# A four-layer graph network on one core: two PSUM slots skipped, sums ordered behind the first pairs, small inputs joined, five checks moved to a later layer

## The chip, the cores and the metric

The kernel runs on one core of a Trainium2 chip. The metric is the device time of one execution in microseconds; the time before is the median of three executions. The profile comes from one further execution, whose own time is given beside its span below.

## What is computed

Four graph layers are applied in turn to 4096 nodes of 64 features with one dense 0/1 matrix `adj` (4096 x 4096, float32). After each layer stands the same residual and normalisation. Cut to what matters:

```python
# layer 0
deg = clip(sum(adj, 1) + 1, 1);  h = (adj @ x + x) / deg
z = relu(concat([x, h]) @ W + b);  out = z / max(norm(z), 1e-12)
# layers 1 and 3 (hyperbolic; c from r, and 1)
left, right = logmap0(x) @ w_att[:D], logmap0(x) @ w_att[D:]
att = sigmoid(left[:, None] + right[None, :] + b_att) * adj
out = proj(expmap(x, einsum('ij,ijd->id', att, logmap(x_i, x_j))))
# layer 2: the last edges of a row weigh 1, 1/2, 1/4, ...
w = mask * 0.5 ** (k - pos);  out = w @ (x @ weight) + bias
# after each: x = layernorm(x + out)
```

## The kernel before

**Tiling.** The host lays `adj` out so that one load (`load(s, g)`, line 718) brings 128 x 2 x 1024 floats, 1 MB: two blocks of 128 neighbours (blocks 2g and 2g+1) for one group `s` of 1024 nodes. There are four groups, `GROUPS` = 3, 2, 1, 0, and sixteen `g` in each, 15 down to 0, so each layer reads 64 MB in 64 loads. All loads are issued by SP's queue into six buffers (`loads`). A buffer is free when TensorE, and the check where there is one, have read it. The matrix products read the upper halves of the floats as bf16.

**Checks.** The fast path holds only if every entry of `adj` is 0 or 1. `check` (line 884, instruction at L886) reads one load on VectorE and counts the entries that are neither. Each of the 64 loads of a sweep is checked once: in layer 0, or, where `checked_later(s, g)` says so, when the same load passes again in layer 2 (`load_2`).

**Layer 0** (from line 1581). For each group, TensorE multiplies each load with the bf16 parts of x (`first`, `third`, L1598) into four accumulators of one PSUM bank each, two `sums` and two `counts`, out of a pool `m0_ps` of six slots. At the group's end `nc.scalar.copy` empties them, in the last group VectorE two of the four (L1628, L1636). What follows for each node (row work) is written as Python generators: `end_0` makes the sums per node by matmuls with `sum_w` and `count_w` (L1544, L1545) and goes on to the normalisation (`norm_rows`) and to what layer 1 needs (`prepare`). `later` puts such a generator into a list, and `tick(n)` moves the lists on by n places, so the row work of one group lies between the pairs of the next. Inside `tc.manual_schedule(engines=FIXED)` TensorE and ScalarE keep the order in which the program names their instructions; VectorE's order is the scheduler's, with row work held behind the checks and pairs before it (`mark`). Outside such blocks the scheduler orders all engines.

**Layers 1 and 3** (`attend`, line 1134). For each block j of 128 neighbours, six matmuls (L1170, L1173, L1176) fill a z tile of two banks, one of three in pool `p_ps`; ScalarE makes the sigmoid (L1190) and a square (L1193), VectorE combines them (L1196 for each block, L1199 for two), and TensorE adds the result up (L1148). Two blocks, one `g`, are called a pair of blocks here. The pool `p_ps` opens when the pools of layer 0 are closed, so its z tiles lie in banks that layer 0 used. In the first sweep of layer 1 the last group's `end_0` runs beside the pairs, partly on GpSimd; the pairs of g = 3 to 0 need its outcome (`need((layer, 2 * g // WB))`). Line 1623 applies a sigmoid to one element, which loads ScalarE's table.

**Layer 2** (`wide_pass`, `narrow_pass`). Groups 3 and 2 are taken at once, then 1, then 0, in fixed order on TensorE and ScalarE. Counting matmuls (L1790), an exponential (L1797) and sums (L1756, L1802) for each block; the checks left from layer 0 run here on VectorE, and so does the row work of `end_2`, `norm_rows` and `prepare` for layer 3, whose results TensorE turns (L1040) and spreads (L1124).

**Small inputs.** Weights and biases come by fourteen transfers from ScalarE's queue near the start: five into `given` (L93), `w0` twice (L96, L1525), two attention rows (L859), `w2` three times (L1613 to L1615), and the rest in a fallback block that is entered only if the checks fail.

Of the kernel before, what the change touches and what calls it, by code (L numbers as in the profile page):

```python
# [10 lines left out]
F32 = mybir.dt.float32  # L11
# [3 lines left out]
AF = mybir.ActivationFunctionType  # L15
# [4 lines left out]
P = 128  # L20
N = 4096
D = 64
NB = N // P
W = 512
# [37 lines left out]
def gnn_stack_kernel(  # L62
# [4 lines left out]
    w0: bass.AP,  # L67
    b0: bass.AP,
    r1: bass.AP,
    w_att1: bass.AP,  # L70
    b_att1: bass.AP,
    w2: bass.AP,
    b2: bass.AP,
    w_att3: bass.AP,
    b_att3: bass.AP,
# [10 lines left out]
    w0_sb = const.tile([2 * D, D], F32, name="w0_sb")  # L86
    w2_sb = const.tile([D, D], F32, name="w2_sb")
# [3 lines left out]
    for src, at in ((b0, 0), (b2, D), (b_att1, 2 * D), (b_att3, 2 * D + 1), (r1, 2 * D + 2)):  # L91
        n = src.shape[0]
        nc.scalar.dma_start(given[:, at : at + n], src.rearrange("(o n) -> o n", o=1))  # L93
    one_row = const.tile([1, P], F32, name="one_row")
    V.memset(one_row, 1.0)
    nc.scalar.dma_start(w0_sb, w0)  # L96
# [475 lines left out]
    def stream(fits):  # L572

        with ExitStack() as st:
# [149 lines left out]
            def checked_later(s, g):  # L724

                return g in (0, 1, 2, 3, 5, 7, 9, 11) or (s in GROUPS[:2] and g in (4, 6))
# [126 lines left out]
            def att_rows(w_att, n):  # L853

                t = att_space[:, n * 4 * D : (n + 1) * 4 * D].rearrange(
                    "o (u k d) -> o u k d", u=2, k=2
                )
                src = w_att.rearrange("(u d) o -> o u d", u=2)
                nc.scalar.dma_start(t, src[:, :, None, :].to_broadcast([1, 2, 2, D]))  # L859
                return t  # L860
# [272 lines left out]

            def attend(layer, s, rate, then):

                left_b = left_bs[s]
# [19 lines left out]
                for g in reversed(range(NB // 2)):  # L1156
# [4 lines left out]
                    for k in (1, 0):  # L1161
# [17 lines left out]
                        if k == 1:  # L1179
# [9 lines left out]
                        sig = sb.tile([P, WW], F32, name="sig", bufs=3)  # L1189
                        nc.scalar.activation(  # L1190
                            sig, left_b, AF.Sigmoid, bias=right[:, j : j + 1]
                        )
# [275 lines left out]
            w2_twice = keep.tile([P, D], F32, name="w2_twice")  # L1468
# [5 lines left out]
            with ExitStack() as lp:  # L1474
# [23 lines left out]
                def constants():  # L1498
# [10 lines left out]
                    V.memset(sum_w[:, D:], 0.0)  # L1509
                    V.tensor_copy(sum_w[D:, :D], w0_sb[D:, :])  # L1510
# [14 lines left out]
                nc.scalar.dma_start(sum_w[:D, :D], w0[D:, :])  # L1525
                att_rows1, att_rows3 = att_rows(w_att1, 0), att_rows(w_att3, 1)
# [5 lines left out]
                def end_0(s, tops):  # L1532
# [3 lines left out]
                    for some in ((0, 1),) if spare else ((0,), (1,)):  # L1536
                        ts = []
                        for h in some:
                            top, low = tops[h]
                            t = take(F32, P, SB, P)  # L1540
                            for k in range(SB):
                                cols = slice(k * P, (k + 1) * P)
                                to = t[:, k, : D + 1]
                                nc.tensor.matmul(to, top[:, cols], sum_w, start=True, stop=False)  # L1544
# [379 lines left out]
```

## Time and profile before

| | us |
|---|---|
| median of three executions | 1049.47 |
| their range | 1048.6 to 1050.73 |
| the profiled execution | 1051.42 |
| its span, first to last instruction | 1049.7 |
| TensorE busy | 977.7 (93%) |
| VectorE busy | 907.8 (86%) |
| ScalarE busy | 751.7 (72%) |
| GpSimd busy | 322.1 (31%) |
| moved by DMA | 271.62 MB |

PE is TensorE, PEld its weight loads, DVE VectorE, ACT ScalarE, POOL GpSimd and SP the engine that issues loads. A "q" behind a name means the engine's sequencer. A row of a group of instructions gives line, engine, operation, output<-inputs, shapes and count, and in brackets how long the engine had been idle and what ended it. A row of windows gives the stretch, its length, each engine's busy time (with instructions), the granted share of TensorE's clock, the share of the DMA engines, and GB/s. The busy share of a whole kernel is an average over four layers with different limits, so most of what follows is read from stretches.

### The profile page before, as it was taken

The page shows a single profiled execution, that of the slowest core. Times are in us where ns is not written, and L with a number is a line of the kernel's source. Part 1 is how long each engine was busy: PE and PEld are TensorE (multiplying, and loading weights), DVE is VectorE, ACT ScalarE, POOL GpSimd, SP SyncE. Part 2 cuts the span into 40 slices and gives each one's busy share as a digit, 9 for nine tenths or more (in the row PEclk, how much of TensorE's full clock was granted, in tenths as well). Part 3 has the DMA queues.
Part 4 walks back from the last instruction along what each step waited for, and adds up shares of the span by engine and source line. Part 5 has one row for each costly group of instructions (what it writes and reads, how often), then busy time and mean ns, then how long its engine had stood idle before and what let it go on. Part 6 is the DMA issues. An engine that isn't in the chain of part 4 may idle for free.

```text
span 1049.7 us, 13606 instructions
## 1 busy us (share of the span) xinstructions
PE 977.7 (93%) x4845; PEld 397.9 (38%) x4845; DVE 907.8 (86%) x1401; ACT 751.7 (72%) x873; POOL 322.1 (31%) x695
## 2 busy tenths in 40 slices
PE   5999997979999999999999999998999999999991
PEld 2455554423333333333333344443333333333330
DVE  7486978789999999999488579858999999999996
ACT  0003123769989888898677688888998898888970
POOL 0011111163055365365210020104501662572660
PEclk9999999999999999999999999999999999999996
DMA  8999999655665566566599998996465666665600
GB/s 339 421 416 407 394 422 381 228 189 177 235 233 203 206 240 208 193 241 229 213 327 353 369 358 308 327 332 231 168 233 199 241 210 205 241 229 186 233 1 24
DMA packets 38580, 271.62 MB, mean 259 GB/s; under 512 B 4710, under 2 KB 4710, under 8 KB 5734
## 3 DMA queue, kind: packets, MB, share of 16 engines
q1 hardware_dynamic: 37728, 270.03, 70.0%
q8 instruction: 40, 0.66, 0.2%
q10 hardware_dynamic: 774, 0.63, 0.2%
q14 instruction: 38, 0.31, 0.1%
HBM read 269.58 MB, written 1.05 MB: 258 GB/s over the span
## 4 chain that ended last, share of the span: by engine, by line
PE 60%; DVE 22%; DMA 6%; POOL 5%; ACT 4%; issue 2%; ACTq 0%; SPq 0%; POOLq 0%; DVEq 0%
PE acc L1148 16%; PE z L1790 11%; PE z L1170 8%; DVE t L1199 7%; PE z L1176 7%; PE z L1173 7%; DVE t L1196 6%; DMA edges<-in_adj_dram 5%; PE z L1802 3%; DVE junk L886 3%; PE acc L1598 3%; PE z L1756 2%; ACT sq L1193 2%; ACT sq L1797 1%; DMA w_twice<-in_L_gnn_weight_dram 1%
## 5 line engine op out<-in xcount | busy, mean ns | idle before, releaser
L1196 DVE SCALAR_TENSOR_TENSOR t<-z,sig 128x1024 f32<-128x1024 f32 x256 | 308.6, 1218 | 24.9 <-ACT sq L1193 22.7
L1193 ACT ACTIVATE sq<-z 128x1024 f32<-128x1024 f32 x256 | 255.5, 1023 | 66.0 <-PE z L1176 31.9
L1199 DVE SCALAR_TENSOR_TENSOR t<-sq,t 128x2048 f32<-128x2048 f32 x127 | 294.5, 2319 | 0.3
L1190 ACT ACTIVATE sig<-left_b,right 128x1024 f32<-128x1024 f32 x256 | 287.0, 1149 | 1.9 <-DVE t L1196 1.0
L1148 PE MATMUL acc<-t,xe 128*64 128x512 f32 x1024 | 255.7, 605 | 16.0 <-DVE t L1199 14.7
L1170 PE MATMUL z<-edges,two_i 128*128 128x512 bf16 x512 | 201.1, 393 | 1.1 <-DVE t L1196 1.1
L1176 PE MATMUL z<-dst,src 74*128 74x512 f16 x512 | 195.1, 381 | 0.0
L1173 PE MATMUL z<-lo_hi,hi_lo 128*128 128x512 f16 x512 | 194.0, 379 | 0.0
L1797 ACT ACTIVATE sq<-z 128x512 bf16<-128x512 f32 (+1 forms) x192 | 138.0, 740 | 39.9 <-PE z L1790 38.7
L1148 PEld LDWEIGHTS acc<-t,xe 128*64 128x64 f32 x1024 | 63.6, 136 | 145.0 <-issue 104.3
L886 DVE SCALAR_TENSOR_TENSOR t<-edges 128x2048 bf16<-128x2048 f32 x36 | 82.4, 2304 | 19.7 <-DMA edges<-in_adj_dram 19.5
L1598 PE MATMUL acc<-edges,first 128*128 128x512 bf16 x256 | 80.2, 394 | 20.5 <-DMA edges<-in_adj_dram 20.0
L1170 PEld LDWEIGHTS <-two_i 128*128 128x128 bf16 x512 | 50.4, 98 | 119.9 <-issue 74.7
L1790 PE MATMUL z<-edges,pass_by 128*128 128x512 bf16 x248 | 86.6, 389 | 6.3 <-ACT sq L1797 5.7
L1790 PE MATMUL z<-edges,enter 128*128 128x512 bf16 x256 | 88.3, 387 | 0.0
L1598 PE MATMUL acc<-edges,third 128*65 128x512 bf16 x256 | 79.5, 391 | 0.0
L1176 PEld LDWEIGHTS <-src 74*128 74x128 f16 x512 | 49.2, 96 | 72.6 <-issue 10.6
L886 DVE SCALAR_TENSOR_TENSOR junk<-edges 128x2048 bf16<-128x2048 f32 x28 | 64.0, 2284 | 11.7 <-DMA edges<-in_adj_dram 11.6
L1173 PEld LDWEIGHTS <-hi_lo 128*128 128x128 f16 x512 | 50.3, 98 | 56.6 <-issue 11.3
L1299 POOL TENSOR_TENSOR w_att<-x,u 128x512 f32<-128x512 f32 x6 | 16.2, 2707 | 149.5 <-ACT u L1293 149.5
L1756 PE MATMUL z<-sq,halves 128*128 128x512 bf16 x128 | 48.0, 377 | 0.2 <-ACT sq L1797 0.2
L1404 ACT COPY x_t<-aux 64x512 f32<-64x512 f32 x8 | 4.6, 576 | 57.5 <-PE aux L1399 57.5
(476 smaller groups left out, 989.4 us busy)
## 6 DMA issues: line engine op xcount, KB each, us to landing
edges<-in_adj_dram SPq DMA_DIRECT2D x256, 1024.0 KB, 4.9
x<-in_x_dram SPq DMA_DIRECT2D x4, 256.0 KB
out_dram<-x ACTq DMA_DIRECT2D x2, 256.0 KB
out_dram<-x SPq DMA_DIRECT2D x2, 256.0 KB
w_sb<-in_L_gnn_W_dram ACTq DMA_DIRECT2D x1, 32.0 KB, 4.8
w_twice<-in_L_gnn_weight_dram ACTq DMA_DIRECT2D x2, 16.0 KB, 7.9
given<-in_L_gnn_b_dram ACTq DMA_DIRECT2D x1, 0.2 KB
given<-in_L_gnn_bias_dram ACTq DMA_DIRECT2D x1, 0.2 KB
```

The lines of the kernel that those rows point to most:

```text
L886: V.scalar_tensor_tensor(junk, a, 0.0, a, ALU.not_equal, ALU.not_equal, accum_out=odd[:, n : n + 1])
L1148: it = nc.tensor.matmul(acc[h * D : (h + 1) * D, :], xe[:, j, :], t[:, k, h * W : (h + 1) * W], start=j == BLOCKS[0], stop=j == BLOCKS[-1],)
L1170: nc.tensor.matmul(half, two_i, edge[:, at : at + W], start=True, stop=False)
L1173: nc.tensor.matmul(half, hi_lo[:, of], lo_hi[:, to], start=False, stop=False)
L1176: last = nc.tensor.matmul(half, src[:, of], dst[:, to], start=False, stop=True)
L1190: nc.scalar.activation(sig, left_b, AF.Sigmoid, bias=right[:, j : j + 1])
L1193: nc.scalar.activation(sq[:, k], zp, AF.Square, bias=ROOT + OFF, scale=-1.0 / UNIT)
L1196: V.scalar_tensor_tensor(ts[k][:, k], zp, 0.0, sig, ALU.max, ALU.mult)
L1199: V.scalar_tensor_tensor(t, sq, HIGH**2, t, ALU.add, ALU.mult)
L1598: nc.tensor.matmul(accs[h][:m], lhs[:, j, :], edge[:, at : at + W], start=j == BLOCKS[0], stop=j == BLOCKS[-1],)
L1790: nc.tensor.matmul(z[:, h : h + W], lhs, rhs[:, h : h + W], start=j == BLOCKS[0], stop=True, skip_group_check=True,)
L1797: weighed[0] = nc.scalar.activation(w, z[:, :n], AF.Exp, bias=-(OFF_EDGE + CUT) * LN2, scale=-LN2)
```

## The change

Four things are done. The first group of layer 0 first takes and gives back two PSUM slots, so that the four accumulators of every group lie two slots further on. In the last `end_0` the first matmul of the sums of each half is ordered behind the last matmul of the pairs traced so far; and the sigmoid of layer 1's first block is made in the last iteration of layer 0, in place of the one-element sigmoid, while `tick` goes five places in the last group. The host joins the weights into one array of 128 x 3 x 64 and the small vectors and attention rows into one row. And `checked_later` sends five more checks to layer 2: g = 8, 6 and 4 of group 0, g = 4 of group 1, and g = 8 of group 2.

```diff
-    for src, at in ((b0, 0), (b2, D), (b_att1, 2 * D), (b_att3, 2 * D + 1), (r1, 2 * D + 2)):
-        n = src.shape[0]
-        nc.scalar.dma_start(given[:, at : at + n], src.rearrange("(o n) -> o n", o=1))
+    nc.scalar.dma_start(given, small[:, : 2 * D + 3])
+    nc.scalar.dma_start(weights_sb, weights)
...
-    nc.scalar.dma_start(w0_sb, w0)
...
-                return g in (0, 1, 2, 3, 5, 7, 9, 11) or (s in GROUPS[:2] and g in (4, 6))
+                more = {0: (4, 6, 8), 1: (4,), 2: (4, 6, 8), 3: (4, 6)}
+                return g in (0, 1, 2, 3, 5, 7, 9, 11) or g in more[s]
...
-                src = w_att.rearrange("(u d) o -> o u d", u=2)
-                nc.scalar.dma_start(t, src[:, :, None, :].to_broadcast([1, 2, 2, D]))
...
+            def sigmoid(layer, s, j):
+
+                early = layer == 1 and j == BLOCKS[0] and s == GROUPS[0]
+                if early:
+                    sig = lefts.tile([P, WW], F32, name="left_b")
+                else:
+                    sig = sb.tile([P, WW], F32, name="sig", bufs=3)
+                nc.scalar.activation(sig, left_bs[s], AF.Sigmoid, bias=right[:, j : j + 1])
+                return sig
...
+                        sig = ahead_of.pop() if ahead_of else sigmoid(layer, s, j)
...
+                    V.tensor_copy(sum_w[:D, :D], weights_sb[:D, 1])
...
-                nc.scalar.dma_start(sum_w[:D, :D], w0[D:, :])
-                att_rows1, att_rows3 = att_rows(w_att1, 0), att_rows(w_att3, 1)
+                nc.scalar.dma_start(att_space, atts_in)
+                att_rows1, att_rows3 = att_rows(0), att_rows(1)
...
+                                one = nc.tensor.matmul(
+                                    to, top[:, cols], sum_w, start=True, stop=False
+                                )
+                                if place[0] == 1 and not k:
+                                    in_order(one.ins, pairs_last[mybir.EngineType.PE])
...
+                        if s == GROUPS[0]:
+                            for _ in range(2):
+                                V.memset(ps.tile([P, W], F32, name="acc")[:1, :1], 0.0)
...
-                                nc.scalar.dma_start(w2_sb, w2)
-                                nc.scalar.dma_start(w2_twice[:D], w2)
-                                nc.scalar.dma_start(w2_twice[D:], w2)
...
-                            tick(4)
+                            if last and g == 0:
+                                ahead_of.append(sigmoid(1, GROUPS[0], BLOCKS[0]))
+                            tick(5 if last else 4)
...
-                            nc.scalar.activation(turned_on, one_row[:, :1], AF.Sigmoid)
```

## The prediction

> **What bounds the kernel now.** I read the slices of the page first, then DMA rate in windows of 5 us, what the load queue (SP) waited for, the timeline where layer 0 turns into layer 1, and last the windows of layer 2.
>
> ```profile
> PE   5999997979999999999999999998999999999991
> DVE  7486978789999999999488579858999999999996
> DMA  8999999655665566566599998996465666665600
> ```
>
> Three regimes: up to slice 7 (layer 0, to 176 us) and again in slices 20 to 27 (layer 2) the DMA share is high; in layers 1 and 3 PE and DVE are both near full and DMA is at six tenths. So a load that comes earlier is worth time in layer 0, a DVE instruction is worth time in layers 1 and 3, and layer 2 (DVE 5 to 9 tenths) has DVE room.
>
> ```profile
> 5.00:10.00 5.00, 3.10 (x8) 1.30 (x9) 4.17 (x8) 0.52 (x1) 0.00 (x0) 1.00 0.86 289
> ...
> 35.00:40.00 5.00, 4.37 (x21) 2.08 (x21) 2.26 (x5) 0.05 (x1) 0.00 (x0) 1.00 1.02 424
> ...
> 80.00:85.00 5.00, 3.76 (x16) 1.54 (x15) 4.89 (x23) 1.66 (x3) 2.40 (x6) 1.00 0.91 338
> ...
> 125.00:130.00 5.00, 3.67 (x16) 1.54 (x15) 4.97 (x11) 0.63 (x2) 1.30 (x4) 1.00 0.97 351
> ...
> 160.00:165.00 5.00, 5.00 (x24) 2.24 (x22) 4.76 (x17) 0.00 (x0) 0.00 (x0) 1.00 0.97 359
> ...
> 180.00:185.00 5.00, 4.37 (x18) 3.56 (x19) 1.19 (x9) 0.59 (x1) 0.00 (x0) 0.55 1.01 426
> ```
>
> The last number is GB/s, the one before the DMA share, before it the granted clock. A good window moves about 420 GB/s. The first 10 us and the windows near 80, 125 and 160 us fall short, and each of the three later ones has DVE at 4.8 to 5.0 of 5. The last row shows PE at clock 0.55: the turn of the layers.
>
> ```profile
> SPq L720 <- DVE junk L886: 93.1, 26, 6.4
> ...
> SPq L720 <- DMA given<-in_L_gnn_b_att_dram: 2.7, 1, 2.7
> SPq L1492 <- DMA xw<-in_L_gnn_att_w_dram: 2.6, 1, 2.6
> SPq L1492 <- DMA given<-in_L_gnn_bias_dram: 2.0, 1, 2.0
> ```
>
> The load queue waits for checks (L886) to free a buffer, and at the start for the landing of small transfers that it has no use for.
>
> ```profile
> 176.56 0.56 ACT L1628 COPY sums<-acc 128x512 f32<-128x512 f32 x1
> ...
> 179.62 0.68 DVE L1628 COPY sums<-acc 128x512 f32<-128x512 f32 x1
> ...
> 180.63 0.66 PE L1544 MATMUL aux<-sum_w,sums 128*128 128x65 f32 x2 [4.11 <-DVE own L1070]
> ...
> 183.65 0.63 PE L1170 MATMUL z<-edges,two_i 128*128 128x512 bf16 x1
> ...
> 187.56 1.23 DVE L1196 SCALAR_TENSOR_TENSOR t<-z,sig 128x1024 f32<-128x1024 f32 x1 [6.33 <-ACT sq L1193]
> ```
>
> PE's layer 0 ends at 176.5. It stands 4.1 us until DVE, held by row work of the group before, has emptied its two accumulators, then does the sums per node, and only at 183.65 the first pair. DVE, which paces layer 1, starts pairs at 187.56.
>
> **The change, part by part.** *Fewer small DMAs.* Five into `given`, two of `w0`, three of `w2`, two attention rows become three (`given`, `weights`, `small`'s rest), all on ACT's queue, where ACT's first instruction is a table load at 9.48. The bytes stay (96 KB of weights), SP's own list of loads too; the fallback block, whose attention loads become four, is not entered. Here a rule speaks against any gain: the Trainium skill, "DMA: Bandwidth & Descriptors", section "Issuing engines are not separate DMA queues", says that transfers from several engines share the same 16 DMA engines and that issuing elsewhere saves only sequencer time. By it the removed issues (0.24 to 0.72 us each in the timeline, on an idle ACT) are worth 0. The rows above differ: SP itself waited 2.0 + 2.7 + 2.6 us for them, its second load went out at 6.75 in place of some 2. I follow the rows. Bytes missing up to 20 us against 420 GB/s, from 2 us on: (420 x 3 − 875) + (420 − 289) x 5 + (420 − 372) x 5 = 385 + 655 + 240 = 1280 KB, or 3.0 us. The cover is the six load buffers: the eleventh load was released by a check at 30.0 us with 6.6 us of transfers still queued, so DVE does not take the place of the DMA. DVE also loses a wait of 1.95 us for `w_twice`, and gains one copy of 0.2 us. I take 2.7 (0 to 3.3).
>
> *Checks moved.* 28 in layer 0 become 23 (group 2 loses g=8, group 1 g=4, group 0 g=8, 6, 4), at 2.29 us each. At 77.6 and 161.0 to 171.1 they are the DVE instruction that releases the next load (issues at 79.94, 163.40, 168.87, 171.21 follow their ends by 0.2 us). Missing bytes: 75 to 85 us 480 KB = 1.1 us; 120 to 130 us 635 KB = 1.5 us, but these hang on the checks of g=8 and 6, which stay, so half; 160 to 174 us some 600 KB = 1.4 us, with a little of the dip before it. Taken: 1.0 + 0.7 + 1.6 = 3.3 us (1 to 5.2). DVE also has the row work of group 1 done 6.9 us sooner, which kept its copies until 179.0. `tick(5)` spreads that row work over 13 places fewer out of 64, about 8 us earlier in PE's and ACT's fixed order; behind it stand the layer's last matmuls. With DVE 6.9 us sooner I cost it at 0, bound 0 to 3 us; its cover is PE's own waits for edges (0.5 us each at 168.3 and 170.8).
>
> *Rotation, order, early sigmoid.* Two one-element memsets (0.06 us each) turn the six accumulators by two, so that the first z tile lies in banks that the last group does not use; the sums per node are ordered behind the last matmul of the first pair. Before: 187.56 − 176.5 = 11.1 us from PE's end to the first L1196. After: PE 6 matmuls at the full-clock step of 0.217 = 1.3 us, with no idle time that lowers the clock; ACT two copies (0.5 each by their steps), one 1.0 us turn copy, one square 1.0 = 3.0 us; DVE two copies 1.4 us. The longest is ACT, 3.0 us: gain 8.0. Edges do not hold it: the first six loads of layer 1 were issued between 169.3 and 175.9, 2.5 us apart in landing against 4.6 us of DVE per pair of blocks (2 x 1.2 + 2.3, the means of L1196 and L1199). The early sigmoid takes its 1.15 us and table load (1.28, already there for `turned_on`) out of this stretch; without it the gain is 6.9 or less. Queued behind the new order: the 16 matmuls of the sums, 3.5 us, and with them the POOL chain that ends with `right` of group 0 at 253 us. They start some 3 us behind the first DVE pair, just as now (190.49 against 187.56), so chain and pairs move together. Taken 8.0 (4 to 9).
>
> *Layer 2 takes five checks*, 5 x 2.29 = 11.5 us of DVE.
>
> ```profile
> 640.00:650.00 10.00, 9.68 (x53) 4.57 (x52) 9.66 (x41) 8.49 (x16) 0.00 (x0) 1.00 0.90 313
> 650.00:660.00 10.00, 8.56 (x49) 4.87 (x47) 8.33 (x23) 8.90 (x17) 0.00 (x0) 1.00 0.82 306
> ...
> 690.00:700.00 10.00, 9.93 (x68) 5.07 (x67) 4.77 (x10) 8.81 (x15) 0.00 (x0) 1.00 0.88 293
> ```
>
> Group 2's goes into 540 to 550, and is caught up by 570, where DVE idles 2.6 us. Group 1's lies ahead of `left` (L1080 at 645.6), which PE needs at 647.43 in its fixed order: 2.3 − 1.6 slack = 0.7 us. Group 0's three, 6.9 us, meet idle times of 2.0 and 5.2 us at 686.9 and 699.4; two lie ahead of L1002 (686.88), which PE needs at 692.48, so 4.6 us against 4.9 of slack. A second rule speaks against the move: "GPSIMD Engine Reference", Key points: POOL contends with a DVE instruction that has two SBUF inputs, as a check has. The chain of waits shows it: `146.70 2.96 POOL sq L1559`, 1.04 when undisturbed, under a check. By the rule each check may hold POOL 2.3 us, 11.5 in all; but POOL's last copies for that turn end at 676.1, 16 us ahead of PE. Taken: 1.0 us lost (0 to 11.5, if cover is gone everywhere).
>
> **Sum.** −2.7 − 3.3 − 8.0 + 1.0 = −13.0 us. The profiled execution took 1051.42 (span 1049.7), 1.95 above the median of 1049.47. So 1038.4 for such an execution and 1036.5 for the median. Layers 1 and 3 keep their pace, so what is won before them stays won.
>
> **Rivals.**
> *The DMA dips only move*: DVE is busy 31.7 of the 35 us from 95 to 130, so earlier loads may wait for the other checks, and group 0's tail or layer 2 gives 2 us more back. Then 1.5 + 1.0 + 8.0 − 2.0 = 8.5: 1041. For it: SP's 93 us behind checks. Against: DVE waits for edges 6.9 us at 93 and 3.2 us at 136, so it has room per group.
> *The rotation frees nothing*, slots being handed out otherwise than in turn: the pairs wait for DVE's copies as now. 6.0 − 1.0 = 5.0: 1044.5. Against: six slots, four per group, are taken in turn if freed in turn.
> *Layer 2's fixed PE order meets late DVE rows*: the full 11.5 us, so 14.0 − 11.5 = 2.5: 1047. It decides once two checks cost their whole length between 630 and 655, where DVE is at 9.5 of 10. Against: PE shows slack of 1.6 and 4.9 us there.
> *Slower: the sums per node slip*. They are behind the pairs now; if they are sent only after more pairs, group 0's rows are late at the 13th pair of the first sweep, which needs them (at 253 now, after 12 x 4.6 = 55 us of pairs and 10 us of DVE idle). Each pair of slip costs 4.6 us; past three it eats the 14 us. At four: 18.5 − 13 = 5.5 slower, 1055. For it: the chain of waits from 200 to 250 runs through POOL. Against: the order names the first pair's last matmul, and only three z tiles exist, so PE has nothing else to send.
>
> **How the numbers follow.** Likeliest 0.62 at 1036.5, its own range 1031 to 1042; dips move 0.16; no rotation 0.08; layer 2 0.07, half of it within 0.2%; slip 0.07. About 0.2%, 2.1 us, is what a measurement here can tell from no change. Faster 0.89, same 0.04, slower 0.07. The range 1030 to 1045 leaves out layer 2's case, the slip and the rims.
>
> **What would show it.** Right: second load issued before 3 us; DMA above 400 GB/s in every window from 5 us to layer 0's end; that end near 170 us; L1170 within 1 us of the last L1598, at full clock, L1544 after it; first L1196 near 173; layer 2's length within 2 us of now; layer 1's from first L1196 unchanged at 320 us. Wrong: a wait of PE at L1124 or L1040 for DVE in layer 2 of several us, a hole of DVE before the 13th pair, or a dip of DMA where g=8 and 6 of group 1 are checked.

## The result and the profile after

The changed kernel takes 1046.37 us (median of 8 runs, 1045.38 to 1048.09) against 1050.1 for the kernel before beside it: ratio 0.9965, 95% interval 0.9955 to 0.9976. A second series gave 0.9951 (0.9938 to 0.9963). So it is faster, by 2.5 to 6.5 us, and not by the 13 that were forecast; 1046.37 lies above the forecast range. The profiled execution took 1045.84 with a span of 1043.7.

The slices of the page, 26.1 us each:

```profile
PE   6899999899999999999999999998999999999991
DVE  7485876799999999999489489979999999999996
DMA  9999999655675566566599999995565665665600
```

PE's two sevens (slices 6 and 8, counted from 0) are nines, slices 1 and 7 went from nine to eight, and the later layers look as before. The windows of layer 0 (the last three columns are granted clock, DMA share, GB/s):

```profile
5.00:10.00 5.00, 0.67 (x2) 0.13 (x2) 2.34 (x9) 0.00 (x0) 0.00 (x0) 1.00 1.00 399
...
80.00:85.00 5.00, 3.06 (x13) 1.23 (x12) 2.47 (x12) 1.43 (x3) 1.84 (x6) 1.00 1.00 415
...
110.00:115.00 5.00, 5.00 (x29) 2.88 (x28) 3.71 (x7) 0.66 (x2) 1.04 (x1) 1.00 0.98 375
115.00:120.00 5.00, 4.93 (x24) 2.29 (x24) 4.90 (x21) 0.00 (x0) 0.00 (x0) 1.00 0.93 362
120.00:125.00 5.00, 4.58 (x33) 2.45 (x32) 4.83 (x14) 1.66 (x3) 0.00 (x0) 1.00 0.90 336
125.00:130.00 5.00, 3.25 (x13) 1.43 (x14) 3.87 (x19) 0.00 (x0) 2.42 (x7) 1.00 0.95 346
...
160.00:165.00 5.00, 4.94 (x29) 2.49 (x28) 4.96 (x31) 1.67 (x4) 2.66 (x7) 1.00 1.01 421
...
180.00:185.00 5.00, 5.00 (x39) 4.06 (x39) 4.43 (x7) 2.07 (x3) 0.00 (x0) 1.00 1.02 424
```

289 GB/s at the start became 399, 338 at 80 us became 415, 359 at 160 us became 421. The dip of group 1 did not go, which the prediction had named as a sign of being wrong: it grew from two windows (362 and 351, with 419 and 421 in the two before them) to the four above. The last load of layer 0 lands at 171.79 instead of 173.62, and PE's last matmul of layer 0 comes 1.9 us sooner instead of 6.

The turn of the layers, from the timeline (start, duration, engine, line; in brackets idle time and what ended it):

```profile
174.06 1.15 ACT L1133 ACTIVATE sig<-left_b,right 128x1024 f32<-128x1024 f32 x1 [3.35 <-PE acc L1602]
174.06 0.69 DVE L1636 COPY u<-acc 65x512 f32<-65x512 f32 x1 [3.82 <-PE acc L1602]
...
175.12 0.99 ACT L1034 COPY lo_hi<-aux 128x1024 f16<-128x1024 f16 x1
176.01 0.58 ACT L1628 COPY sums<-acc 128x512 f32<-128x512 f32 x1
176.48 0.58 ACT L1636 COPY w_att<-acc 65x512 f32<-65x512 f32 x1
...
177.12 0.39 PE L1170 MATMUL z<-edges,two_i 128*128 128x512 bf16 x1 [2.21 <-ACT w_att L1636]
...
178.91 1.02 ACT L1190 ACTIVATE sq<-z 128x1024 f32<-128x1024 f32 x1
...
179.97 1.23 DVE L1193 SCALAR_TENSOR_TENSOR t<-z,left_b 128x1024 f32<-128x1024 f32 x1 [4.62 <-ACT sq L1190]
```

DVE's two copies now stand directly at PE's end (174.06; 179.02 before). But the first z tile is not free: PE waits 2.21 us for ACT's second copy, which stands behind a sigmoid and a turn copy. The first pair starts at 179.97 instead of 187.56, so 7.6 us sooner; at the end of the first two blocks (first L1196, 186.26 against 192.90 for the same instruction) 6.6 are left, through layers 1 to 3 they vary between 4.7 and 6.8, and the span is 6.0 shorter. The medians show 3.7: the two profiled executions differ by 5.6, and that of before lay 1.3 above the median of its companions, that of after 0.5 below.

Layer 2 with its five further checks:

```profile
640.00:650.00 10.00, 8.49 (x43) 4.17 (x42) 9.86 (x32) 8.52 (x17) 0.00 (x0) 1.00 0.91 319
650.00:660.00 10.00, 9.94 (x60) 5.48 (x60) 8.00 (x29) 8.61 (x15) 1.04 (x1) 1.00 0.87 312
...
690.00:700.00 10.00, 9.95 (x56) 4.58 (x56) 6.32 (x16) 8.93 (x15) 0.00 (x0) 1.00 0.93 338
```

DVE is at 9.86 of 10, and PE at 8.5 to 10: the layer is 0.5 us shorter, not 1.0 longer.

### The profile page after: what moved, and what is told of

Its sections match the earlier page's. It is cut to its first block, busy times and chain, and to the rows that moved or that the text cites. A ratio compares the mean times of both kernels' runs of the same rounds, so it can differ in the third digit from the quotient of the medians.

```text
span 1043.7 us, 13511 instructions
## 1 busy us (share of the span) xinstructions
PE 969.8 (93%) x4759; PEld 397.0 (38%) x4845; DVE 906.7 (87%) x1404; ACT 751.8 (72%) x872; POOL 332.5 (32%) x695
## 4 chain that ended last, share of the span: by engine, by line
PE 56%; DVE 15%; POOL 5%; ACT 4%; issue 2%; ACTq 0%; POOLq 0%; DVEq 0%
PE acc L1148 16%; PE z L1790 11%; PE z L1173 7%; PE z L1176 7%; PE z L1170 7%; DVE t L1196 7%; DVE t L1193 6%; PE z L1802 3%; PE z L1756 2%; ACT sq L1190 1%; ACT sq L1797 1%; PE aux L1279 1%; PE aux L1114 1%; ACT sig L1133 1%; POOL rb L969 0%
## 5 line engine op out<-in xcount | busy, mean ns | idle before, releaser
L1193 DVE SCALAR_TENSOR_TENSOR t<-z,sig 128x1024 f32<-128x1024 f32 x255 | 307.3, 1217 | 17.2 <-ACT sq L1190 15.0
L1196 DVE SCALAR_TENSOR_TENSOR t<-sq,t 128x2048 f32<-128x2048 f32 x127 | 294.4, 2318 | 0.3
L1170 PE MATMUL z<-edges,two_i 128*128 128x512 bf16 x462 | 181.4, 393 | 7.8 <-DVE t L1193 5.6
L1148 PEld LDWEIGHTS acc<-t,xe 128*64 128x64 f32 x1024 | 64.0, 136 | 141.3 <-issue 105.8
L876 DVE SCALAR_TENSOR_TENSOR t<-edges 128x2048 bf16<-128x2048 f32 x41 | 94.0, 2308 | 18.8 <-DMA edges<-in_adj_dram 18.8
L1602 PE MATMUL acc<-edges,first 128*128 128x512 bf16 x241 | 76.9, 395 | 16.9 <-DVE first L1491 9.3
L1790 PE MATMUL z<-edges,enter 128*128 128x512 bf16 x247 | 85.4, 387 | 0.4
L876 DVE SCALAR_TENSOR_TENSOR junk<-edges 128x2048 bf16<-128x2048 f32 x23 | 52.5, 2284 | 15.0 <-DMA edges<-in_adj_dram 15.0
L1560 POOL TENSOR_TENSOR sq<-z 128x512 f32<-128x512 f32 x4 | 10.0, 2491 | 122.2 <-DVE z L1558 101.5
```

What stands on the lines that cost most here:

```text
L876: V.scalar_tensor_tensor(junk, a, 0.0, a, ALU.not_equal, ALU.not_equal, accum_out=odd[:, n : n + 1])
L1148: it = nc.tensor.matmul(acc[h * D : (h + 1) * D, :], xe[:, j, :], t[:, k, h * W : (h + 1) * W], start=j == BLOCKS[0], stop=j == BLOCKS[-1],)
L1170: nc.tensor.matmul(half, two_i, edge[:, at : at + W], start=True, stop=False)
L1193: V.scalar_tensor_tensor(ts[k][:, k], zp, 0.0, sig, ALU.max, ALU.mult)
L1196: V.scalar_tensor_tensor(t, sq, HIGH**2, t, ALU.add, ALU.mult)
L1602: nc.tensor.matmul(accs[h][:m], lhs[:, j, :], edge[:, at : at + W], start=j == BLOCKS[0], stop=j == BLOCKS[-1],)
```

## Experiments

Diffs are against the changed kernel unless said otherwise. "Before" in a ratio is always the kernel before on the same chip; series on different chips are compared by their ratios. A profile is one execution, and where it lies far from its median this is said. Loads are counted from 1 here; the expectations' 8th, 31st and 47th are the 9th, 32nd and 48th. The tables and the differences of landings come from the loads' and instructions' records in the traces.

**Parts taken alone or back: joined inputs, checks, rotation.**

```diff
 e_joined_only: the kernel before, with the joined inputs
 e_checks_back:
-  more = {0: (4, 6, 8), 1: (4,), 2: (4, 6, 8), 3: (4, 6)}
+  more = {0: (), 1: (), 2: (4, 6), 3: (4, 6)}
 e_no_rotation:
-  for _ in range(2):
-      V.memset(ps.tile([P, W], F32, name="acc")[:1, :1], 0.0)
 e_no_checks0:
-  if not checked_later(s, g):
+  if not checked_later(s, g) and g < 0:
...                                  # and odd, which the checks fill, is set to 0
```

> The kernel before with the joined inputs alone (checks, rotation, order, sigmoid, ticks as before). My forecast's term: 2.7 us, so 1047.4 against 1050.1, with PE's layer 0 ending 2.7 us sooner. Rival A, the start is worth what the landings of the changed kernel show (#8 came 1.2 us sooner, #31 1.3): 1.2 to 1.9 us, 1048.5. Rival B, the rule that an issue on another queue costs only sequencer time: 0, 1050.1, landings of #8 and #31 unmoved. Tells: landing of the 8th and 31st load, end of the last L1602-like matmul.

Measured: 1049.17, ratio 0.9992 (0.9979 to 1.0006). The second load goes out at 2.18 us, and the 16th, 32nd and 64th load land 1.75, 1.8 and 1.85 us sooner than before. So 1.8 in the trace, as rival A had it, and 0.8 with 1.4 either way in the time: my 2.7 lies outside, rival A and the rule's 0 inside the interval. The landings of one program scatter (against the second profile of before, below, it would be 3.1 us at the 9th load and 5.8 at the 64th), so the time decides.

> The changed kernel with no check in layer 0 at all (23 left out, their part of the result is not computed). If the checks still gate the loads in the changed kernel, layer 0 runs at the DMA rate of a good window: 68.2 MB at 420 GB/s is 162.4 us, from 2 us on with 10 us of landing of what is queued, so PE's last L1602 ends at 166 to 169 in place of 174.0. If the loads are at their floor already (start and rate, not checks), it ends at 172.5 or later.

Measured in a single execution: 1045.28, span 1043.6, the same as the changed kernel. DMA has no dip left:

```profile
80.00:85.00 5.00, 4.51 (x21) 1.99 (x20) 0.00 (x0) 0.00 (x0) 0.00 (x0) 1.00 1.01 411
120.00:125.00 5.00, 5.00 (x36) 2.77 (x35) 0.00 (x0) 0.00 (x0) 0.00 (x0) 1.00 1.01 419
125.00:130.00 5.00, 4.61 (x26) 2.25 (x26) 0.00 (x0) 0.64 (x1) 0.00 (x0) 1.00 1.01 418
```

Even so the last load lands at 170.09, and PE's layer 0 ends at 172.1: the changed kernel stood within 1.7 us of the floor. To leave the start out, I take the time from the 9th landing to the 64th. It is 139.3 us here, 141.9 in the kernel before, and 141.7 with the joined inputs alone. So all the checks of layer 0 together had cost some 2.5 us of landing in these two executions. In the second profile of before, whose dips are deeper (285 GB/s at 80 us, 213 at 160 us), the stretch takes 144.4 us, so 5.1. Five executions of the changed layer 0 (two of the changed kernel, and those without rotation, order and early sigmoid) have 140.1 to 141.3.

> The changed kernel with the five checks back in layer 0. My forecast's terms: layer 0 longer by 3.3 us, layer 2 shorter by 1.0, so 1046.4 + 2.3 = 1048.7. Rival A (the dips only move, the moved checks were worth 0.5 us or less and layer 2 nothing): 1046.4 to 1046.9, PE's layer 0 ends within 0.5 us of 174.0. Rival B (group 1's row work, late again under the checks, holds DVE's two evacuation copies as before): first L1193 later by 3 us or more beside that of PE's end.

Measured: 1049.8, ratio 0.9998 (0.9982 to 1.0014): the whole gain is gone, 3.4 us. But not by the loads: the last one lands at 171.04, sooner than in the changed kernel's own profile, and the 9th to the 64th take 140.5. Its profiled execution took 1046.85, 2.9 below the median, and shows a part of the loss: PE's layer 0 ends 2.3 us later than in the changed kernel, and every pair of layer 1 comes 2.3 us later; the turn itself is as short (6.1 us), so rival B fell. PE waits in its fixed order for row work that DVE has not reached (waits of PE, 155 to 180 us):

```profile
PE aux L1029 <- DVE ys L991: 2.7, 1, 2.7
PE z L1169 <- ACT w_att L1635: 2.2, 1, 2.2
```

> The changed kernel without its two one-element memsets, so that the six accumulators fall as before: the first z tile then lies on the bank of sums 0 (ACT copies it first) and that of counts 1 (DVE, ended 175.35 in the changed kernel). With the two memsets it lies on sums 1 and counts 0 (ACT's second copy, 177.1), so it is not clear of the last group as my forecast had it. Forecast's theory (rotation frees the first z tile): without it the pairs start later, by 2 us or more, 1048.5. New theory (it frees nothing, ACT's copies are waited for in both): first L1170 0.5 us sooner, first L1193 0 to 0.5 sooner, 1045.9 to 1046.4.

Measured: 1045.97, ratio 0.997 (0.996 to 0.9981), the same as with it. The first pair waits for the same copy as long, 2.21 us:

```profile
176.50 0.39 PE L1170 MATMUL z<-edges,two_i 128*128 128x512 bf16 x1 [2.21 <-ACT w_att L1633]
177.98 0.63 PE L1170 MATMUL z<-edges,two_i 128*128 128x512 bf16 x1
```

The rotation frees nothing. In each run with this wait but e_tick4 the first z tile starts with the last of the four evacuation copies, ACT's here and DVE's in e_turn_only; whether the slots are not handed round in turn, as my forecast had assumed, or the new pool waits for all of them, is not shown.

**The turn of the layers, one part taken back at a time.**

```diff
 e_tick4:
-  tick(5 if last else 4)
+  tick(4)
 e_no_order:
-  if place[0] == 1 and not k:
-      in_order(one.ins, pairs_last[mybir.EngineType.PE])
 e_late_sigmoid:
-  ahead_of.append(sigmoid(1, GROUPS[0], BLOCKS[0]))   # in the last iteration
+  nc.scalar.activation(turned_on, one_row[:, :1], AF.Sigmoid)   # ahead of the copies
 e_checks7:
-  1: (4,)
+  1: (4, 6, 8)
```

> The changed kernel with tick(4) in the last group too. My forecast put tick(5) at 0: 1046.4, first L1193 at about 180.0 as in the changed kernel. New theory: tick(5) is a main source of the gain at the turn of the layers, because it takes group 1's row work out of DVE's last microseconds of layer 0, so that DVE's two evacuation copies (174.06 and 174.67 in the changed kernel, 179.02 and 179.62 before) no longer hold the bank of the first z tile. By it the copies fall behind row work again, near 177 to 178, and first L1193 comes 2 to 5 us later: 1048.5 to 1051. Rival: tick(5) costs time, since it puts the turn copies L1034 ahead of ACT's evacuation copies; then first L1193 comes 1 to 2 us sooner, 1045.

Measured: 1045.26, ratio 0.9953 (0.9936 to 0.9969). No loss: DVE's copies start at 172.69 and 173.29, first L1193 at 178.50. The new theory of this expectation fell. So did its rival, that tick(5) costs time, though the first L1193 did come 1.5 us sooner: the 2 us that the first two blocks were ahead were gone by the 7th pair.

> The changed kernel without the ordering of the sums per node behind the first pair. They then stand where the planner puts them, which before was half of them ahead of the first pair: 8 matmuls of 0.22 each at full clock or 0.43 at half clock, 1.8 to 3.5 us, and DVE's rows of them ahead of the first L1193. Expected first L1193 2 to 4 us later than 179.97, 1048.5 to 1050.5. Rival (the sums only change places with the pairs that wait behind them, the end of pair 2 is the same): 1046.4 to 1047.

Measured: 1045.73, ratio 0.9957 (0.9941 to 0.9972). No loss either. On every engine the instructions ran in the same order as with it: the planner puts the sums behind the first pair without being told.

> The changed kernel with the first sigmoid back in layer 1 and `turned_on` back in front of the copies. Forecast: first L1193 later by up to 1.1 us, 1046.4 to 1047.6. ACT's queue from PE's end to the first square is 5.0 us already in the changed kernel (174.06 to 178.91), so one sigmoid more is on the path: +1.1. Rival (the planner had two sigmoids in front of the first square in either kernel and takes one away here): 0.

Measured: 1045.96, ratio 0.9961 (0.9949 to 0.9972). First L1193 comes 7.2 us behind PE's last layer 0 matmul instead of 6.1, as the forecast had it, but at the end of the first two blocks the distance is the same within 0.3 us.

> The changed kernel with the checks g=8 and 6 of group 1 moved to layer 2 as well. Theory: the only dip of DMA that makes loads land later is that of group 1 (the 47th load lands at 131.1 in the changed kernel, 129.35 without any check). Then the last load lands 1.2 to 1.7 us sooner (171.8 to some 170.3), PE's layer 0 ends at some 172.5, and what is left of it behind the turn depends on PE's clock there (0.57 in 176 to 178 us without any check): 1045 to 1046.4; two checks more in layer 2 cost 0 to 0.5. Rival (the dip moves on to another group's checks): last load at 171.5 or later, 1046.4 to 1047.

Measured: 1055.01, ratio 1.0048 (1.0029 to 1.0066), slower than before. Layer 0 does what the theory said: the 48th load lands at 128.62, the last at 169.34, and 9th to 64th take 139.3 us, the floor. The pairs of layer 1 are 0.9 us ahead. Then layer 2 loses 10 us at one place (first the wait row of PE, then its timeline):

```profile
PE acc L1114 <- DVE left L1070: 7.7, 1, 7.7
```

```profile
648.14 1.11 PE L1114 MATMUL acc<-ident,left 128*128 128x128 f32 x4 [7.69 <-DVE left L1070]
649.05 0.63 PE L1790 MATMUL z<-edges,pass_by 128*128 128x512 bf16 x1
```

In the changed kernel `left` (L1070) was done at 638.94 and PE came for it at 641.05: 2.1 us were left, no wait. Two checks more on DVE, 4.6 us, and the row work that follows them came 9 us later; what made 9 of 4.6 is not shown. So the rival of layer 2's fixed order was at the right place (L1114); it decides between five checks and seven.

**Which parts carry the gain.** With no single part of the turn worth anything that shows, I took them all away.

```diff
 e_joined_checks, joined_checks_again: joined inputs and the five checks alone
   (no memsets, no in_order, `turned_on` as before, tick(4))
 e_turn_only: joined inputs, rotation, order, early sigmoid; checks as before, tick(4)
 e_copies_first:
-  tick(5 if last else 4)
+  if not (last and g == 0):
+      tick(5 if last else 4)
```

> The kernel before with the joined inputs and the five moved checks alone: no memsets, no order, no early sigmoid, tick(4). My forecast gives these two parts 2.7 + 3.3 - 1.0 = 5.0 us (1045.1) and the rest 8.0 more. By the forecast the pairs wait as before at the turn, so this kernel is some 8 us slower than its own 1036.5, or by what the changed kernel measured, 1046.4 plus what the turn is worth there (5.7 us to the first L1193): 1050 or more. New theory: the first sweep is not paced by its first pair but by the chain of row work on POOL from the sums per node to `right` of group 0 (L1072 at 246.86 in the changed kernel, 252.98 before), and undoing any one of the parts at the turn moved the time by less than 1 us; the sums per node here still stand half in front of the pairs, early. Then 1045.5 to 1048, with `right` between 246 and 250.

Measured: 1044.4, ratio 0.9939 (0.9921 to 0.9958). All the parts at the turn are gone, and the kernel is not slower.

> Joined inputs with the rotation, the order and the early sigmoid, but the checks where they were and tick(4): the turn's parts without the moved checks and without tick(5). Forecast: 1046.4 + 2.3 = 1048.7 at the scale of the changed kernel, with the first L1193 3 us behind PE's end. New theory: what counts is when `right` of group 0 is done; with five checks more ahead of group 1's row work on DVE the sums and their rows come later than in the changed kernel, 1047 to 1049, but sooner than with tick(5) and the checks back (1049.8), since tick(4) leaves that row work behind PE's last matmuls in the fixed order.

Measured: 1048.12, ratio 0.9983 (0.9972 to 0.9993): without the moved checks the turn's parts give 0.9 us over the joined inputs alone, with intervals that overlap. In the profiled execution they do more:

```profile
176.17 0.69 DVE L1627 COPY sums<-acc 128x512 f32<-128x512 f32 x1
176.77 0.68 DVE L1635 COPY u<-acc 65x512 f32<-65x512 f32 x1
...
177.51 0.40 PE L1169 MATMUL z<-edges,two_i 128*128 128x512 bf16 x1 [2.12 <-DVE u L1635]
...
180.15 1.23 DVE L1192 SCALAR_TENSOR_TENSOR t<-z,left_b 128x1024 f32<-128x1024 f32 x1 [1.78 <-ACT sq L1189]
```

DVE's copies still come 1.6 us behind PE's end (174.6), but the first pair stands ahead of the sums and starts 5.6 us behind that end, against 11.3 with the joined inputs alone; from the third pair on all pairs are 3.4 us ahead of those of e_joined_only. So the turn's parts shorten the turn too. This execution took 1046.18, 1.9 below its median, and that of e_joined_only lay 1.3 above its own; why the other executions do not show the gain is open.

> The kernel before once more, for the scatter between profiled executions of one program. Landings of the 8th, 48th and 64th load within 0.7 us of 31.7, 133.5 and 173.6, `right` of group 0 within 1 us of 252.98, span within 2 us of 1049.7.

Measured: 1055.37, span 1053.6, 4 us longer than its first profile, all of it ahead of the end of layer 0 (last load at 177.57). The expectation of 2 us was too narrow: the runs of before reach from 1046.4 to 1055.0 in one series. From the first pair to the end the two profiles run parallel within 0.2 us.

> The changed kernel with the row work of the last place of layer 0 (two turn copies of 1.0 us on ACT) behind the evacuation copies. Theory of the first look at the traces: ACT's turn copy ahead of the evacuation copies holds the first z tile (2.21 us of wait at L1170), so first L1170 0.9 to 1.9 us sooner. Rival: ACT does the same two turn copies and one sigmoid ahead of the first square all the same, so the first L1193 stays within 0.5 us. By the chain theory the time follows `right` of group 0: the sums per node read what ACT copies and come behind the first pair, so 0 to 1.5 us sooner: 1045 to 1046.4.

Measured: 1045.41, ratio 0.9955 (0.9938 to 0.9972). The first pair starts at 178.05, and the first two blocks end 9.1 us sooner than before, 2.4 sooner than in the changed kernel. The lead lasts for twelve pairs; at the 17th 0.9 us over the changed kernel are left, at the 41st none. The pairs from the 13th on need group 0's rows, and the last instruction of `right` (L1072) starts at 248.08, 1.2 us later than in the changed kernel.

**On one chip, and the last open points.**

```diff
 e_chain_short:
-  nc.gpsimd.tensor_mul(sq, z, z)
+  sq = z                             # group 0 only
 e_jc_wait2: joined inputs and five checks, and
-  later(end_0(GROUPS[-1], tops), False, 4)
+  later(end_0(GROUPS[-1], tops), False, 2)
 e_jc_g0: joined inputs and group 0's three checks   more = {0: (4, 6, 8), 1: (), 2: (4, 6), 3: (4, 6)}
 e_jc_g12: joined inputs and the other two           more = {0: (), 1: (4,), 2: (4, 6, 8), 3: (4, 6)}
```

> The changed kernel without one POOL instruction of the chain, the squares of group 0's rows ahead of their norm (L1560, 2.95 us; the sum is taken of the rows themselves, so the norm is another number and the result too). Chain theory: DVE's wait at L1562 (0.9) goes, its wait at L929 for POOL (4.0 in the changed kernel) shrinks by some 2 to 3 us, every later pair of the first sweep comes as much sooner, `right` at 244 to 245, time 1043.5 to 1044.5. Rival (the places in the fixed order set the pace, POOL is hidden): `right` and time unchanged within 0.5 us, 1046.4.

Measured: 1044.85, ratio 0.994 (0.9925 to 0.9955). In the trace the pairs gain 1.0 us at the third pair (the wait at L1562 is gone), and the wait at L929 stays:

```profile
DVE n_m L929 <- POOL z L1570: 4.0, 1, 4.0
```

So the 2.95 us instruction was worth 1.0; the rest was hidden, since DVE's next row instruction keeps its place among the pairs. The theory that POOL's chain paces the whole first sweep fell in this form.

> Joined inputs and moved checks alone, with the sums per node and their row work called for two ticks sooner (2 in place of 4 in the queue of row work, so one block sooner). Chain theory: the rows of group 0 reach POOL one block, some 2.5 us, sooner against the pairs; what of it the waits at L929 take back is open: 1042 to 1044.4. Rival (given back at DVE's waits for POOL in full, as the three us that the copies placed first had won): 1044.4, or slower by the longer wait.

Measured: 1046.6, ratio 0.9962 (0.9949 to 0.9974), 2 us slower than with 4 ticks. DVE's wait at L929 is unchanged at 2.3, but the pairs fall behind at the seventh and eleventh. Called sooner, the row work only waits at other places.

> The changed kernel once more, beside the next one on the same chip. 1046 to 1046.5; in the trace the last load of layer 0 within 0.7 us of 171.1, L929's wait for POOL 4.0 us.

> Joined inputs and moved checks alone, beside the changed kernel on the same chip. If the rotation, the order, the early sigmoid and tick(5) together give nothing or cost something: 0 to 2 us faster than the changed kernel. If the 1044.4 of its first runs was scatter: 1045.5 to 1047.

Measured: 1046.02 and 1044.58, ratios 0.9951 (0.9938 to 0.9963) and 0.9945 (0.9933 to 0.9957). The changed kernel's landing (170.60) and wait (4.0) are as expected. On this chip joined inputs and checks alone are 1.4 us below the changed kernel; the intervals of the ratios overlap, so: not slower, likely some 1.5 us faster.

> Joined inputs, and of the five checks only group 0's three moved to layer 2; nothing of the turn's parts. Theory: the moved checks win at the turn, not in the loads: with three checks fewer at the end of layer 0, DVE has group 1's row work done before PE's last matmul, and its two evacuation copies and L1060 no longer hold PE (4.1 us before, 1.0 with all five moved). Then nearly all of the gain of the five is here: 1044.5 to 1046, DVE's copies within 1 us of PE's end. Rival (the gain is the sum of loads that come sooner over all groups): about half of it, 1047 to 1048.

> The complement: joined inputs, and only the check g=8 of group 2 and g=4 of group 1 moved. By the theory 0 to 1 us better than the joined inputs alone, 1048 to 1049.5, with DVE's evacuation copies 3 us or more behind PE's end as before. Rival (loads): the other half, 1047.

Measured: 1044.47, ratio 0.9939 (0.9923 to 0.9955), and 1049.91, ratio 0.9996 (0.9983 to 1.0009). Group 0's three checks carry the whole gain of the five, the other two nothing that can be told from noise. With the joined inputs they make the version with the least code, faster than before and not slower than the changed kernel, whose intervals touch or overlap its own. In e_jc_g12 DVE's copies come 2.1 us behind PE's end, less than the 3 expected. Their timelines at the turn, e_jc_g0 first:

```profile
173.11 0.69 DVE L1632 COPY u<-acc 65x512 f32<-65x512 f32 x1 [5.53 <-PE acc L1598]
...
174.73 0.41 PE L1541 MATMUL aux<-sum_w,sums 128*128 128x65 f32 x2 [1.02 <-DVE own L1060]
...
176.31 0.39 PE L1170 MATMUL z<-edges,two_i 128*128 128x512 bf16 x1
...
178.94 2.50 DVE L1193 SCALAR_TENSOR_TENSOR t<-z,sig 128x1024 f32<-128x1024 f32 x2 [3.62 <-ACT sq L1190]
```

```profile
175.29 0.17 DVE L1068 TENSOR_TENSOR f<-f,m 128x8 f32<-128x8 f32 x1
175.37 0.68 DVE L1632 COPY u<-acc 65x512 f32<-65x512 f32 x1
...
176.98 0.66 PE L1541 MATMUL aux<-sum_w,sums 128*128 128x65 f32 x2 [2.87 <-DVE own L1060]
177.44 0.63 PE L1544 MATMUL aux<-count_w,u 65*128 65x65 f32 x2
...
183.90 1.23 DVE L1193 SCALAR_TENSOR_TENSOR t<-z,sig 128x1024 f32<-128x1024 f32 x1 [6.33 <-ACT sq L1190]
```

And the window of e_jc_g12 behind its wait, with the clock granted:

```profile
178.00:180.00 2.00, 2.00 (x12) 2.00 (x12) 0.00 (x0) 0.17 (x1) 0.00 (x0) 0.50 1.04 438
```

The ends of PE's layer 0 differ by 0.4 us only. With the three checks moved, DVE stood idle for 5.5 us and copies at once; without, it is still in group 1's row work (L1068) and copies 2.3 us later. PE then waits 2.9 us instead of 1.0, and its matmuls go to half clock (0.50 granted; the rows of two follow each other after 0.43 us instead of 0.22): from the first sum to the first L1193 it is 6.9 us in place of 4.2. Sum: 0.4 + 1.9 + 2.7 = 5.0 us, the difference of the two first L1193. These two kernels differ in all five checks. Two other pairs differ in group 0's three alone, and agree: e_jc_g0 is at its first L1193 6.6 us ahead of the joined inputs, and the two executions with all five checks are 3.3 and 4.7 us ahead of e_jc_g12. The half clock is not bound to the checks: it came in the first of those two executions as well (next table).

| us | PE's layer 0 ends | DVE's copies start | first L1193 | end of first L1196 |
|---|---|---|---|---|
| before | 175.7 | 179.02 | 187.56 | 192.90 |
| joined inputs | 174.3 | 177.05 | 185.58 | 190.50 |
| joined inputs and the turn's parts (e_turn_only) | 174.6 | 176.17 | 180.15 | 184.97 |
| the changed kernel with the checks back | 176.1 | 177.03 | 182.22 | 188.51 |
| with checks of groups 2 and 1 | 173.3 | 175.37 | 183.90 | 188.96 |
| with checks of group 0 | 172.9 | 173.11 | 178.94 | 183.77 |
| with all five checks, first series | 173.0 | 173.21 | 180.61 | 185.50 |
| with all five checks, second series | 173.1 | 173.34 | 179.16 | 183.98 |
| the changed kernel | 173.9 | 174.06 | 179.97 | 186.26 |
| the changed kernel, second profile | 172.7 | 172.86 | 178.77 | 186.70 |

("With checks" means joined inputs and these checks moved. PE's end is the start of its last layer 0 matmul and one step of 0.22 us; the 176.5 of the prediction counts the turn matmuls behind it too. L1193 and L1196 are the changed kernel's names; the other kernels have the same instructions under other numbers.)

## Why the prediction was right and wrong

**The direction** was right, the size off by 10 us. By kernels, taking ratios times 1050: joined inputs −0.8 (0.9992), moved checks −5.3 more (to 0.9942, the mean of two series), rotation, order, sigmoid and tick(5) on top of these +1.7 (to 0.9958, the mean of two). Forecast: −2.7, −2.3 with layer 2 in it, −8.0. By stretches of the two first profiles: 1.9 us were won up to PE's end (forecast 6.0) and 5.7 in the turn (forecast 8.0), and 1.5 of these 7.6 were given back within the first seven pairs. Two steps failed, the division by 420 and the work credited with the turn; both follow below.

**Fewer small DMAs, 2.7: mis-sized.** The bytes missing in the first 20 us were there as computed (289 to 399, 372 to 423 GB/s), but 3.0 us of bytes were 1.6 us at the 9th landing (30.10 for 31.68), 1.85 at the last, and 0.8 in the time. (The load released at 30.0 us was the twelfth, not the eleventh.)

**Checks in layer 0, 3.3: the failed step is "missing bytes divided by 420 GB/s".** The dips of the kernel before, 4.0 us by that division, had cost 2.5 us of landing (5.1 in the second execution, whose windows from 30 to 170 us fall short of 420 GB/s by 8.9 us, where those of the first fall short by 5.0), and moving five checks won about 1 of it: 140.1 to 141.3 us from the 9th to the 64th landing with the checks moved, 140.5 to 141.9 in the first profile of before and in the three kernels with joined inputs and the checks in place (e_joined_only, e_turn_only, e_checks_back). The dips moved: group 1's grew from 1.5 to 3.1 us of missing bytes (375, 362, 336 and 346 GB/s from 110 to 130 us). With the start this makes some 2.7 us in place of 6.0, what the rival "the dips only move" had (2.5). Moved bytes are not landed loads: at its last landing the kernel without checks had moved 70.1 MB, the kernel before 68.7, and layer 0 needs 68.2. What is above is of layer 1's loads, which were already issued. The Trainium skill, "DMA: Bandwidth & Descriptors", section "Why a DMA increments its semaphore by 16 and not by 1", says that a transfer runs on up to 16 engines that finish independently. That in a dip only the engines that were ahead ran dry would fit, but the traces don't name a packet's engine, so this stays open. A PE end near 170 was not to be had: without a single check it is 172.1.

**The same checks at the turn, 0 in my sum: some 5 us, the second failed step.** I had the mechanism in hand: "DVE also has the row work of group 1 done 6.9 us sooner, which kept its copies until 179.0". I used it only to cost tick(5) at 0, and booked PE's 4.1 us of wait and its half clock under the rotation and the order alone. The moved checks remove that wait by themselves.

**Rotation, order, early sigmoid, 8.0: not needed beside the moved checks, and mis-sized.** The stretch did shrink from 11.8 to 6.1 us (PE's last matmul to first L1193), but to 6.0 in the kernel with group 0's checks moved and none of these parts, and to 5.6 in the profile of e_turn_only, with these parts and no check moved. Each way shortens the turn, and both together no further; in the time only the checks pay in full (0.9939 against 0.9983). The size failed at ACT, to which I gave 2.0 us between PE's end and the first square: it did 5.0 us of work there, two sigmoids, two turn copies and the two evacuation copies. "The first z tile lies in banks that the last group does not use" was wrong (2.21 us of wait in either case); the early sigmoid takes 1.1 us off ACT ahead of the first pair and nothing two blocks later; the order changed no order. What the parts did together: in e_jc_g0 a first part of the sums runs at 174.73 to 176.3, while ACT does a turn copy and sigmoids; in the changed kernel all sixteen stand behind the first pair (179.76 to 183.28), with three row instructions of DVE ahead of its second L1193. First L1193 to the end of the first L1196 is 6.3 us there and 4.8 in e_jc_g0, whose lead over before then stays at 9.1 us while that of the changed kernel falls to 6.1. No single part puts the sums back in front; which two or three of them together do was not tried.

**tick(5), 0 with bound 0 to 3:** 0 where the checks are moved (e_tick4). With the checks back it looks 1.6 us slower (0.9998 less 0.9983, times 1050; the intervals overlap), and PE waits 2.7 us at L1029 for DVE: the "cover" that mattered was DVE being early.

**Layer 2, +1.0 (0 to 11.5):** 0, so the low end: from its first counting matmul to the first pair of layer 3 it takes 198.5 us before, 198.0 in the changed kernel and 198.5 with the joined inputs and five checks alone. The slack of 1.6 us at `left` was read rightly, but the check ahead of it did not eat it: 2.1 us are left in the changed kernel. The bound was worth keeping: with two checks more the stretch takes 207.9 us.

**Rivals.** "The rotation frees nothing" was right that nothing is freed, wrong about its price, since the wait for DVE went with the moved checks. "Sums slip" did not come: `right` of group 0 moved with the pairs, 252.98 to 246.86.

## What to carry to other kernels

When an engine waits for another at a change of stage, ask what the late engine was doing, and book the gain to whatever takes that work away; here moving three checks of 2.29 us in the last group was worth all of it, and the code written for the turn added nothing to that. Two changes that remove the same wait do not add up, so each is to be tried without the other. A dip in the summed DMA rate is not lost time in full: compare landings, and first make a kernel without the suspected work to see the floor. Before moving work under "slack" in a fixed order, write down the slack of each instruction that another engine will come for, and again after each step: with five checks 2.1 us were left, with seven layer 2 lost 10 us.

## What the runs showed of the hardware

The same program at the same place ran at full clock in one execution and at half in another. PE waits 2.21 us for ACT's copy in both (changed kernel, first and second profile; the column before the last two is the granted clock):

```profile
176.00:178.00 2.00, 0.82 (x3) 0.39 (x4) 0.00 (x0) 2.00 (x5) 0.00 (x0) 1.00 1.00 418
178.00:180.00 2.00, 1.99 (x11) 1.10 (x11) 0.03 (x1) 2.00 (x3) 0.00 (x0) 1.00 1.01 422
```

```profile
176.00:178.00 2.00, 2.00 (x8) 0.79 (x8) 0.00 (x0) 2.00 (x3) 0.00 (x0) 0.81 1.00 418
178.00:180.00 2.00, 2.00 (x7) 0.97 (x5) 1.23 (x1) 1.77 (x2) 0.00 (x0) 0.50 1.01 422
180.00:182.00 2.00, 2.00 (x18) 2.00 (x17) 0.00 (x0) 1.02 (x1) 0.00 (x0) 0.84 0.99 414
```

The second had PE's end 1.2 us sooner, and its first two blocks ended 0.4 us later: the clock took 1.6 us. The joined inputs with all five checks show the same: PE waits 1.02 us in both executions, and in the first the clock is at 0.52 and 0.63 in the windows from 176 to 180 us, in the second at 1.00, and the first L1193 comes 1.6 us later behind PE's end. The Trainium skill, "TensorE: Matmul & The Clock Gate", section "What's actually happening", has a window of some 3.4 us that runs free of the kernel, so that it is chance where a wait falls in it. That agrees: in the rows above the clock is at half for 3.4 us in all (0.81, 0.50 and 0.84 of 2 us each), and one program met it in one execution and not in the other. But the page puts half clock behind at least one idle window of that length, and here it came behind waits of 2.2 and of 1.0 us, so the measurement decides. The half clock also took back what the kernel without checks had won: 0.57 from 176 to 178 us there.

The scatter of whole runs goes with group 0's checks: with them in layer 0 it is 1046.4 to 1055.0 (before, 28 runs), 1047.7 to 1052.2 (e_jc_g12, 14 runs) and 1045.9 to 1051.2 (e_turn_only, 20 runs, although its turn is short in the profile); with them moved and nothing else at the turn 1043.2 to 1045.7 (18 runs). Why is not shown.
